# Layer 2's harmonics transposed two groups ahead, and a prologue that loads its edges by group

## The chip, the cores and the metric

The kernel runs on one core of a Trainium2 chip. The core has five engines with an instruction queue each: TensorE (PE, matmuls and transposes, with weight loads PEld beside them), VectorE (DVE), ScalarE (ACT), GpSimd (POOL) and SyncE (SP, which here only issues DMAs). The time is the device time of one execution in microseconds, as a median over runs. Besides, one execution was recorded by the hardware profiler; every single duration below is from that execution.

## The reference

Four graph layers run one after the other on the same graph: N = 12500 nodes of 128 features, E = 212500 edges, sorted by destination. Each layer takes h = relu(layernorm(x)) and adds its result to x.

```python
def reference(x, src, dst, edge_attr_16, edge_attr_9, edge_weight, edge_weight1, ...):
    h = jnp.maximum(_layernorm(x), 0.0)
    x = x + _L0(h, edge_index, edge_attr_16, ...)
    h = jnp.maximum(_layernorm(x), 0.0)
    x = x + _L1(h, edge_index, edge_weight1, ...)
    h = jnp.maximum(_layernorm(x), 0.0)
    x = x + _L2(h, edge_attr_9, edge_index, ...)
    h = jnp.maximum(_layernorm(x), 0.0)
    x = x + _L3(h, edge_index, ...)
    return x

# layer 0: attention. Wh = h @ W.T in 4 heads of 32
attn = leaky_relu((concat(Wh[src], Wh[dst]) * a).sum(-1)) + edge_feat @ W_e.T
alpha = softmax of attn over the edges of each dst
out = layernorm(gelu(segment_sum(alpha * Wh[src], dst)))
# layer 1: gelu(gelu(segment_sum(h[src] * edge_attr, dst)) @ W.T + b)
# layer 2: tensor product with 9 spherical harmonics per edge, five paths (i1, i2, io)
tmp = einsum('eui,ej,ijk->euk', x1[i1], x2[i2][:, 0, :], CG[p])
msg = einsum('euk,uw->ewk', tmp, weights[p]) * alpha
out = zeros.at[dst].add(msgs)
# layer 3: mean of relu(h)[src] over each dst, two matmuls, batch norm over the nodes
```

In layer 2 the node row of 128 is one block of 32 scalars and one of 32 vectors of 3.

## The kernel before

The edges are cut into NG = 208 groups of GE = 1024, each as 128 partitions with T = 8 slots. Because the edges are sorted by destination, a group's destinations lie in a short window of nodes. A group is summed by a one-hot matrix: `rel` is the destination less the group's first one (`base`), the one-hot compares it with the columns 0 to 127, held in PSUM as `iop` (L176 to L178), and a matmul with the one-hot as one operand adds the edges' rows into the window's nodes. An edge's source row is fetched by an indirect DMA on POOL's queue, one per slot, so 8 per group (`gather`, L730; L738 is a variant that spaces them out, used in layers 1 and 3).

**Prologue.** The table loop (from L238) normalizes x in 25 batches of rows, transposes them on PE (L252), multiplies by `WE` (L260) and writes table `tab0`, from which layer 0 gathers; `rows0` loads the batches eight ahead into nine buffers of `xt`. `sdall` becomes the table `sdt` (L276 and the store ahead of it). Then the edges: `load_edges` (L123) brings dst and src into [partition, group, slot], 8 indices of 4 bytes in each piece (`di`, `si`). Extremes of each group come from reductions over the slots and a reduction over the partitions on POOL (L331), and from them `base`, `rel` (L335) and several index tables. `dpad` is a padded copy of dst in DRAM, read back as `seq` in shifted rows, which gives the sortedness check `bad` and the unit counts `units` (matmul `pun`, L386). `rough` (L402) collects whatever would break the kernel's assumptions. Last, `rel16`, a copy of `rel` in group order and bf16, is made by 13 transposes (L408), 13 copies and 13 stores (L411). Weights follow (L424, L429, L446).

**Layer 0.** Its loop does for a group `load` (the edge features, `rb` from rel16 L1019, `sdw` from sdt L1023), `logits` (gather into X, one of LAG + 8 = 15 buffers; transpose of the features L1032, copy eT L1034, matmuls, the logit sums), and LAG groups later, after the softmax over windows (`weights`), `spread_out` (msg L1112, matmuls L1116) and `add_up` (L1120).

**Layer 2.** The order is written out by hand (`tc.manual_schedule`). Per group: `mix` transposes the 9 harmonics of 8 slots on PE (pyT, L1334), copies them on ACT (eT, L1336) and multiplies by `mixer` on PE (mix, L1337), which gives 15 coefficients per edge. `window2` is a generator that is advanced step by step: 8 scalings on ACT (A, L1350); the one-hot on DVE (L745); 8 tensor operations on DVE with the coefficients (L1355 to L1367, called BC here); 8 matmuls on PE (pag, L1372) and the copy R on ACT (L1374); 3 transposes on PE (pT, L1377); the addition into acc on DVE (L1380). Iteration g issues mix(g+1), then for its own group the gathers, A, the one-hot and BC, then acc(g-3), pag and R of g-1, and pT of g-2. X has 11 buffers; `py`, with both the transposed harmonics and the coefficients, has 2. `Nodes` adds, every other group or so, the node work of finished windows (L590 to L622). So on PE the order is pyT(g+1), mix(g+1), pag(g-1), pT(g-2); on ACT eT(g+1), A(g), node work, R(g-1).

`feature_stream` (L798) holds the edge features in blocks of 4 groups and loads a block when its first group asks for it:

```python
            if b not in held:
                held.clear()
                g1 = min((b + 1) * per, NG)
                held[b] = sp.tile([P, per, T * k], F, name=name)
                load_edges(held[b], v, b * per, g1, 0.0, k)
```

Of the kernel before, what the change touches and what calls it, by code (L numbers as in the profile page):

```python
# [26 lines left out]
P = 128  # L27
T = 8
# [65 lines left out]
def gnn_kernel(ctx: ExitStack, tc, x, src, dst, ef16, ef9, ew, W0, We0, a0, lns, lnb, W1, b1,  # L94
# [81 lines left out]
    cps = ctx.enter_context(tc.tile_pool(name="cps", bufs=1, space=PSUM))  # L176
    iop = cps.tile([P, W], F, name="iop")
    vec.tensor_copy(iop, io)  # L178
# [24 lines left out]
    tmp = early.enter_context(tc.tile_pool(name="acp", bufs=1))  # L203
    sp, pp = (pre.enter_context(p) for p in (tc.tile_pool(name="p0", bufs=3),
# [3 lines left out]
    def rows0(k):  # L208
        if k < NK:
            b0, nb = k * NBK, min(NBK, NB - k * NBK)  # L210
            xs0[k] = sp.tile([P, nb, D], F, name="xt", bufs=9)
            load_rows(xs0[k], x, b0, nb)

    NK = -(-NB // NBK)
    for k in range(8):
        rows0(k)
    with tc.tile_pool(name="wt0", bufs=1) as wp, tc.tile_pool(name="wtp0", bufs=1, space=PSUM) as pw_:
# [13 lines left out]
        vec.tensor_copy(WE[:, P:], aps)  # L231
    sdall = sp.tile([P, NB, H], F, name="sdall", bufs=1)
    for k in range(NK):
# [19 lines left out]
        hT = sp.tile([P, nb, P], F, name="hT")  # L253
# [10 lines left out]
        rows0(k + 8)  # L264
# [14 lines left out]
    si = cst.tile([P, NG, T], I, name="si")  # L279
# [12 lines left out]
    TOT = PADF + NG * GE + P  # L292
# [6 lines left out]
    with tc.tile_pool(name="ed", bufs=1) as ep:  # L299
        di = ep.tile([P, NG, T], I, name="di")  # L300
        load_edges(di, dst, 0, NG, N, 1)
        load_edges(si, src, 0, NG, 0, 1)
        df = ep.tile([P, NG, T], F, name="df")
        vec.tensor_copy(df, di)

        ends = ep.tile([1, max(PADF, TOT - PADF - E)], I, name="ends")
        vec.memset(ends, -1)
        nc.sync.dma_start(dpad[None, :PADF], ends[:, :PADF])
        ends2 = ep.tile([1, TOT - PADF - E], I, name="ends2")
        vec.memset(ends2, N)  # L310
        nc.sync.dma_start(dpad[None, PADF + E :], ends2)
        cut = max(k for k in range(1, P + 1) if E % k == 0)
        nc.sync.dma_start(dpad[PADF : PADF + E].rearrange("(a b) -> a b", a=cut), dst.rearrange("(a b) -> a b", a=cut))
        ext = ep.tile([P, 2, NG + 1], F, name="ext")
        vec.memset(ext[:, :, NG:], 0.0)
        vec.tensor_reduce(ext[:, 0, :NG], df, AX.X, ALU.max)
        vec.tensor_reduce(ext[:, 1, :NG], df, AX.X, ALU.min)
        vec.tensor_scalar_mul(ext[:, 1, :NG], ext[:, 1, :NG], -1.0)

        seq = [ep.tile([P, NG * T], I, name=f"seq{k}") for k in (0, 1, 2)]  # L320
        for t, k in zip(seq, (0, 1, HALO)):
            nc.sync.dma_start(t, windows(dpad, PADF + k, P, NG * T, NG * T))
        bad = [ep.tile([P, NG * T], F, name=f"bad{k}") for k in (0, 1)]
        vec.tensor_tensor(bad[0], seq[2], seq[0], ALU.is_le)
        vec.tensor_scalar(bad[1], seq[0], float(N), None, op0=ALU.is_lt)
        vec.tensor_tensor(bad[0], bad[0], bad[1], ALU.mult)
        vec.tensor_tensor(bad[1], seq[1], seq[0], ALU.is_lt)
        vec.tensor_tensor(bad[0], bad[0], bad[1], ALU.max)
        vec.tensor_reduce(ext[:, 0, NG:], bad[0], AX.X, ALU.max)
        red = ep.tile([P, 2, NG + 1], F, name="red")  # L330
        pool.partition_all_reduce(red, ext, P, bass_isa.ReduceOp.max)  # L331
        base = ep.tile([P, NG], F, name="base")
        vec.tensor_scalar_mul(base, red[:, 1, :NG], -1.0)
        vec.tensor_copy(bi, base)
        vec.tensor_tensor(rel, df, base[:, :, None].to_broadcast([P, NG, T]), ALU.subtract)  # L335
        vec.tensor_scalar(widx, base, pcol, None, op0=ALU.add)
        span = ep.tile([P, NG], F, name="span")
        vec.tensor_tensor(span, red[:, 0, :NG], base, ALU.subtract)
        vec.tensor_copy(xall, span)
        vec.tensor_scalar(xall, xall, 7, None, op0=ALU.logical_shift_right)  # L340
        vec.tensor_scalar(xall, xall, 1.0, None, op0=ALU.add)
        vec.tensor_scalar(bi3, base, float(BM), None, op0=ALU.min)
        vec.tensor_scalar(bir, bi, RW - 1, None, op0=ALU.bitwise_and)

        last = base[:, G0 - GM : G0, None].to_broadcast([P, GM, T])
        vec.tensor_tensor(relx, rel[:, G0 - GM : G0, :], last, ALU.add)
        vec.tensor_scalar(relx, relx, W0_ * P - 0.5, 4.0 * P, op0=ALU.is_gt, op1=ALU.mult)
        vec.tensor_tensor(relx, relx, rel[:, G0 - GM : G0, :], ALU.add)
        most = ep.tile([P, 1], F, name="most")
        vec.tensor_reduce(most, span, AX.X, ALU.max)  # L350
        worst = ep.tile([P, 1], F, name="worst")
        vec.scalar_tensor_tensor(worst, red[:, 0, NG:], float(W), most, op0=ALU.mult, op1=ALU.max)

        least = ep.tile([P, NG], F, name="least")
        pool.memset(least, 0.0)
        for k, g in enumerate(done):
            if g + 1 < NG:
                pool.memset(least[:, g + 1 :], float(min(NBK * P * (k + 1), N)))
        pool.memset(least[:, G0:], float(W0_ * P))
        for k, g in enumerate(done):  # L360
            if g + 1 >= G0 and g + 1 < NG:
                pool.memset(least[:, g + 1 :], float(min(NBK * P * (k + 1), N)))
        vec.tensor_tensor(least, base, least, ALU.is_lt)

        end = ep.tile([P, NG], F, name="end")
        pool.memset(end, float(RW - W))
        for k, g in enumerate(done):
            if g + 6 < NG:
                pool.memset(end[:, g + 6 :], float(NBK * P * (k + 1) + RW - W))
        vec.tensor_tensor(end, base, end, ALU.is_gt)  # L370
        vec.tensor_tensor(least, least, end, ALU.max)

        UP = NG * T // P
        edge = ep.tile([P, 2, NW], F, name="edge")
        vec.tensor_copy(edge[:, 0, :], wnode)
        vec.tensor_scalar(edge[:, 1, :], wnode, float(P), float(N), op0=ALU.add, op1=ALU.min)
        below = ep.tile([P, 2, NW, UP], F, name="below")
        for k, at in enumerate((P - 1, 0)):
            unit = seq[0].rearrange("p (u e) -> p u e", e=P)[:, :, at]
            vec.tensor_tensor(below[:, k], unit[:, None, :].to_broadcast([P, NW, UP]),  # L380
                              edge[:, k, :, None].to_broadcast([P, NW, UP]), ALU.is_lt)
        units = ep.tile([P, 2, NW], F, name="units")
        vec.tensor_reduce(units, below, AX.X, ALU.add)
        with tc.tile_pool(name="bgp", bufs=1, space=PSUM) as pp:
            pun = pp.tile([P, 2, NW], F, name="pun")
            pe.matmul(pun.rearrange("p k w -> p (k w)"), ones, units.rearrange("p k w -> p (k w)"),  # L386
                      start=True, stop=True)
            vec.tensor_scalar(begin, pun[:, 0, :], float(P), float(E - UN * P), op0=ALU.mult, op1=ALU.min)
            vec.tensor_copy(units[:, 1, :], pun[:, 1, :])
            vec.tensor_tensor(units[:, 0, :], units[:, 1, :], pun[:, 0, :], ALU.subtract)  # L390
        vec.tensor_scalar(units[:, 0, :], units[:, 0, :], UN + 0.5, None, op0=ALU.is_gt)
        many = ep.tile([P, 1], F, name="many")
        vec.tensor_reduce(many, units[:, 0, :], AX.X, ALU.max)
        vec.scalar_tensor_tensor(worst, many, float(W), worst, op0=ALU.mult, op1=ALU.max)
        vec.tensor_scalar(many, base[:, G0 - 1 : G0], BM + 0.5, None, op0=ALU.is_gt)
        vec.scalar_tensor_tensor(worst, many, float(W), worst, op0=ALU.mult, op1=ALU.max)
        vec.tensor_scalar(many, red[:, 0, G0 - GM - 1 : G0 - GM], W0_ * P - 0.5, None, op0=ALU.is_gt)
        vec.scalar_tensor_tensor(worst, many, float(W), worst, op0=ALU.mult, op1=ALU.max)
        late = ep.tile([P, 1], F, name="late")
        vec.tensor_reduce(late, least, AX.X, ALU.max)  # L400
        vec.scalar_tensor_tensor(worst, late, float(W), worst, op0=ALU.mult, op1=ALU.max)
        vec.tensor_copy(rough, worst)  # L402
        relf = rel.rearrange("p g t -> p (g t)")
        with tc.tile_pool(name="edp", bufs=2, space=PSUM) as pp:
# [587 lines left out]
    with (tc.tile_pool(name="e0", bufs=2) as sp, tc.tile_pool(name="e0p", bufs=2, space=PSUM) as pp,  # L992
# [129 lines left out]
        with tc.manual_schedule():  # L1122
# [46 lines left out]
            while nodes.step(NG + LAG + 2):  # L1169
                pass  # L1170
            slots.close()


    def tabled1(sp, pp, tabS, make):

# [645 lines left out]
```

## Time and profile before

| what | us |
|---|---|
| median of 4 runs | 9673.07 (9665.19 to 9674.17) |
| the profiled execution | 9670.84 |
| its span | 9669.0 |
| prologue, to the first gather of layer 0 | 170.6 |
| layer 0, to its last pag | 3368.7 |
| layer 1 and what lies between | to about 5150 |
| layer 2 | about 5150 to 7966 |
| layer 3 | the rest |
| busy: PE, PEld, DVE, ACT, POOL | 5156.2, 3242.7, 5346.7, 2808.2, 5146.3 |

The span is read in order of time. The stages follow each other, since each gathers from the table that the one before wrote. No engine is busy for more than 55% of the span (DVE), so a share over the whole span does not name a bound; each stage is read by itself, by its waits and its timeline. In the lists below a line of a timeline is: start, duration (us), engine, line, operation, out<-in, shape, count, and in brackets the idle time of the engine just ahead and what ended it. A line of a wait list is: engine, tile and line that waited, <- what released it: us in total, times, longest. "remote" stands for a releaser that the records do not explain. SPq is the DMA queue that SP issues to.

### The profile page before, as it was taken

How to read it: one execution, taken by the hardware profiler on the slowest of the kernel's cores; microseconds unless marked ns; L12 is line 12 of the kernel's file. 1: busy time of each engine (PE TensorE's matmuls, PEld its weight loads, DVE VectorE, ACT ScalarE, POOL GpSimd, SP SyncE). 2: the span in 40 equal slices, each digit the busy share in tenths (PEclk: the TensorE clock that was granted, in tenths of full speed). 3: DMA queues.
4: the chain of work that ended last, by engine and by line, in shares of the span. 5: the costliest groups of instructions: out<-in, count | busy, mean ns of one | idle time of the engine just before them, and what ended most of it. 6: DMA issues, size and time to landing. Idle time of an engine off the chain costs nothing. (4 is left out here: it accounts for less than half of the span.)

```text
span 9669.0 us, 105443 instructions
## 1 busy us (share of the span) xinstructions
PE 5156.2 (53%) x33167; PEld 3242.7 (34%) x33168; DVE 5346.7 (55%) x10302; ACT 2808.2 (29%) x7509; POOL 5146.3 (53%) x5434
## 2 busy tenths in 40 slices
PE   2233333333333328788883555555555564777776
PEld 2233333332333215555552333333333331222222
DVE  4465665665566613334343777777777772444443
ACT  2133332333333303333332222222222221333333
POOL 2554555555545166666634555555555526665662
PEclk6565555555556658888886777777777786888887
DMA  7232222232223222222221111111111114333333
GB/s 104 64 76 71 75 74 73 74 76 72 73 72 77 48 78 72 75 76 76 74 64 52 45 52 51 50 55 50 51 52 51 53 32 121 87 88 84 87 88 91
DMA packets 740838, 673.63 MB, mean 70 GB/s; under 512 B 340899, under 2 KB 629014, under 8 KB 740247
## 3 DMA queue, kind: packets, MB, share of 16 engines
q0 software_dynamic: 186624, 382.17, 15.0%
q1 hardware_dynamic: 553643, 284.63, 11.7%
q8 instruction: 262, 4.29, 0.2%
q14 instruction: 309, 2.53, 0.1%
HBM read 603.91 MB, written 63.28 MB: 69 GB/s over the span
## 5 line engine op out<-in xcount | busy, mean ns | idle before, releaser
L730 POOL DMA_INDIRECT X<-tab,si x1664 | 1615.5, 971 | 1463.4 <-DVE msg L1112 676.3
L730 POOL DMA_INDIRECT X<-htab,si x1664 | 1576.3, 947 | 1131.4 <-ACT prods L1350 583.6
L738 POOL DMA_INDIRECT X<-htab,si x968 | 939.9, 971 | 630.4 <-PE pag L1309 219.0
L738 POOL DMA_INDIRECT xg<-tab,si x968 | 921.1, 952 | 649.5 <-issue 230.2
L1372 PE MATMUL pag<-prods,oh 128*128 128x352 f32 x3328 | 1237.4, 534 | 0.0
L1116 PE MATMUL pag<-oh,msg 128*128 128x128 f32 x3328 | 724.9, 406 | 328.8 <-DVE msg L1112 277.9
L1372 PEld LDWEIGHTS pag<-prods,oh 128*128 128x128 f32 x3328 | 739.9, 229 | 411.3 <-issue 180.0
L1337 PE MATMUL py<-mixer,eT 72*128 72x120 f32 x416 | 131.3, 408 | 1234.2 <-ACT eT L1336 1066.6
L1116 PEld LDWEIGHTS pag<-oh,msg 128*128 128x128 f32 x3328 | 671.5, 308 | 344.2 <-DVE msg L1112 281.4
L1510 ACT CAST xb<-px 128x384 bf16<-128x384 f32 x1050 | 491.8, 480 | 1006.2 <-PE px L1499 337.2
L1036 PE MATMUL pt<-WeB,eT 128*128 128x32 f32 x416 | 124.2, 390 | 1108.0 <-ACT eT L1034 815.6
L1246 ACT ACTIVATE xs<-px,wslot 128x128 f32<-128x128 f32 x1050 | 371.4, 366 | 1150.2 <-PE px L1234 474.8
L1374 ACT COPY R<-pag 128x352 f32<-128x352 f32 x208 | 94.1, 452 | 1905.6 <-remote 1223.4
L1234 PE MATMUL px<-tabS,oha 128*32 128x128 f32 x8652 | 518.4, 315 | 212.9 <-issue 108.3
L1499 PE MATMUL px<-tabS,oha 128*32 128x384 bf16 x4326 | 441.8, 395 | 305.2 <-issue 195.7
L1215 PE MATMUL pw<-ohb,xs 128*128 128x128 f32 x2100 | 578.7, 362 | 18.8 <-ACT xs L1246 12.5
L1309 PE MATMUL pag<-oh,X 128*128 128x128 f32 x1936 | 443.7, 319 | 213.3 <-issue 123.0
L1337 PEld LDWEIGHTS py<-mixer,eT 72*128 72x128 f32 x416 | 82.9, 249 | 1295.2 <-ACT eT L1336 1108.5
L1350 ACT ACTIVATE prods<-X,ef 128x128 f32<-128x128 f32 x1664 | 510.3, 393 | 12.4 <-DMA X<-htab,si 12.1
L1036 PEld LDWEIGHTS pt<-WeB,eT 128*128 128x128 f32 x416 | 97.1, 290 | 1183.1 <-ACT eT L1034 865.5
L1380 DVE TENSOR_TENSOR acc<-acc,pT 128x384 f32 x208 | 114.5, 550 | 678.9 <-remote 655.0
L1105 ACT ACTIVATE oh<-iop,far 128x128 f32<-128x128 f32 x1664 | 452.9, 383 | 41.1 <-DVE ohj L948 32.7
(463 smaller groups left out, 10265.9 us busy)
## 6 DMA issues: line engine op xcount, KB each, us to landing
lob<-lo SPq DMA_DIRECT2D x252, 224.0 KB
rb<-rel SPq DMA_DIRECT2D x208, 256.0 KB
X<-htab,si POOLq DMA_INDIRECT x2632
X<-tab,si POOLq DMA_INDIRECT x1664
xtab<-xv SPq DMA_DIRECT2D x72, 256.0 KB
xv<-xtab SPq DMA_DIRECT2D x72, 256.0 KB
xg<-tab,si POOLq DMA_INDIRECT x968
lob<-lo SPq DMA_DIRECT2D x84, 160.0 KB
```

Source lines behind the costliest of these rows:

```text
L730: pool.indirect_dma_start(out=t[:, s, :], out_offset=None, in_=table[:, :], in_offset=bass.IndirectOffsetOnAxis(ap=idx[:, s : s + 1], axis=0))
L738: pool.indirect_dma_start(out=ts[-1][:, : table.shape[1]], out_offset=None, in_=table[:, :], in_offset=bass.IndirectOffsetOnAxis(ap=idx[:, ...
L1105: act.activation(S[:, t, :], iop, AF.Abs, bias=far[:, t : t + 1])
L1116: pe.matmul(pag, msg[:, t, :], S[:, t, :], start=t == 0, stop=t == T - 1)
L1215: pe.matmul(pw, x, b, start=j == 0, stop=j == NT - 1)
L1234: pe.matmul(px[q * SL : (q + 1) * SL, :], a[:, jj * P + q * SL : jj * P + (q + 1) * SL], tabS[:, blk, :], start=True, stop=True)
L1246: act.activation(x, px, AF.Copy, scale=by)
L1309: pe.matmul(p, r[t], s[:, t, :], start=t == 0, stop=t == T - 1)
L1350: act.activation(A[:, t, :], X[:, t, :], AF.Copy, scale=e[:, t, 0:1])
L1372: pe.matmul(pag, S[:, t, :], prods[:, t, :], start=t == 0, stop=t == T - 1)
L1499: pe.matmul(px[q * SL : (q + 1) * SL, :], a[:, jj * P + q * SL : jj * P + (q + 1) * SL], tabS[:, blk, :], start=True, stop=True)
L1510: act.copy(x[:, : 3 * P], px)
```

## The change

Four parts.

1. **Layer 2.** `mix` becomes a generator `turn` of three steps: transpose, copy, matmul. Iteration g now does the matmul of g+1, whose transpose and copy are done already, then the transpose of g+2, and, as its last step behind R(g-1), the copy of g+2. `py` gets three buffers. The PSUM for it comes from `iop`, which is closed for this layer and put beside `part` (the products in BC) in one PSUM tile `own`; it is made again ahead of layer 3.
2. **Prologue.** dst and src are loaded as rows of one group each (4 KB) in [112 | 96 x 1024], turned into slots on PE (`slots_of`), src ahead of the table loop, dst behind it. Extremes are reductions over the row, spread to all partitions by a matmul of ones with a diagonal (`pr`). `rel16` is written by two stores from ACT's casts. The padded copy is stored first; the sortedness check works in bf16 and stands last. The x ring has 7 buffers, loaded six ahead.
3. **Layer 0's X** has a pool of its own (`xr`), made ahead of the prologue's pools and closed behind layer 0.
4. **`feature_stream`** loads a block of four groups ahead (layers 0 and 2).

The diff, cut to its core:

```diff
@@ constants @@
-    cps = ctx.enter_context(tc.tile_pool(name="cps", bufs=1, space=PSUM))
-    iop = cps.tile([P, W], F, name="iop")
-    vec.tensor_copy(iop, io)
+    held_ = ctx.enter_context(ExitStack())
+    def columns(name):
+        t = held_.enter_context(tc.tile_pool(name=name, bufs=1, space=PSUM)).tile([P, W], F, name="iop")
+        vec.tensor_copy(t, io)
+        return t
+    iop = columns("cps")
...
+    rows_ = ExitStack()
+    xr = rows_.enter_context(tc.tile_pool(name="xr", bufs=LAG + 8))
...
-            xs0[k] = sp.tile([P, nb, D], F, name="xt", bufs=9)
+            xs0[k] = sp.tile([P, nb, D], F, name="xt", bufs=7)
...
-    for k in range(8):
+    for k in range(6):
         rows0(k)
@@ ahead of the table loop @@
+    gd = [ep.tile([n, GE], I, name=f"gd{c}") for c, n in enumerate(HN)]
+    gs = [ep.tile([n, GE], I, name=f"gs{c}") for c, n in enumerate(HN)]
...
+    for t, v in ((gs, src), (gd, dst)):
+        m = HN[1] // 16 * 16 - 16
+        for c, a, b in ((0, 0, HN[0]), (1, 0, m), (1, m, HN[1] - 1)):
+            nc.sync.dma_start(t[c][a:b], v[(HB[c] + a) * GE : (HB[c] + b) * GE].rearrange("(g e) -> g e", g=b - a))
+        nc.sync.dma_start(t[1][HN[1] - 1 : HN[1], :tail], v[None, (NG - 1) * GE :])
+    def slots_of(out, t, c):
+        n = HN[c]
+        for q in range(0, T, 4):
+            ps = ppt.tile([P, 4, HN[0]], F, name="pst")[:, :, :n]
+            for k in range(4):
+                pe.transpose(ps[:, k, :], t[:, q + k :: T], ident[:n, :n])
+            vec.tensor_copy(out[:, HB[c] : HB[c + 1], q : q + 4].rearrange("p g t -> p t g"), ps)
...
+    for c in (0, 1):
+        gsf = ep.tile([HN[0], GE], F, name="gf", bufs=2)[: HN[c]]
+        vec.tensor_copy(gsf, gs[c])
+        slots_of(si, gsf, c)
@@ behind the table loop @@
-        load_edges(di, dst, 0, NG, N, 1)
-        load_edges(si, src, 0, NG, 0, 1)
...
-        pool.partition_all_reduce(red, ext, P, bass_isa.ReduceOp.max)
...
-                pe.transpose(prl[:n, :], relf[:, c : c + n], ident)
-                rl = ep.tile([P, P], B16, name="rl", bufs=2)
-                vec.tensor_copy(rl[:n, :], prl[:n, :])
-                nc.sync.dma_start(rel16[c : c + n, :], rl[:n, :])
...
+        for c in (0, 1):
+            vec.tensor_copy(gf[c], gd[c])
+            n = HN[c]
+            vec.tensor_reduce(ext[:n, c, 0:1], gf[c], AX.X, ALU.min)
+            vec.tensor_reduce(ext[:n, c, 1:2], gf[c], AX.X, ALU.max)
+            for k in (0, 1):
+                dg = ep.tile([P, P], F, name="dg", bufs=2)[:n, :n]
+                vec.tensor_scalar(dg, ident[:n, :n], ext[:n, c, k : k + 1], None, op0=ALU.mult)
+                pe.matmul(pr[:, k, HB[c] : HB[c + 1]], ones[:n, :], dg, start=True, stop=True)
+            vec.tensor_scalar(gf[c], gf[c], ext[:n, c, 0:1], None, op0=ALU.subtract)
+        vec.tensor_copy(red, pr)
...
+        act.copy(r16, gf[c].rearrange("g (p t) -> g t p", t=T))
+        nc.sync.dma_start(rel16[HB[c] * T : HB[c + 1] * T, :].rearrange("(g t) p -> g (t p)", t=T),
+                          r16.rearrange("g t p -> g (t p)"))
+        slots_of(rel, gf[c], c)
...
+        pe.matmul(pbd, ones, anybad, start=True, stop=True)
@@ feature_stream @@
-            if b not in held:
-                held.clear()
-                g1 = min((b + 1) * per, NG)
-                held[b] = sp.tile([P, per, T * k], F, name=name)
-                load_edges(held[b], v, b * per, g1, 0.0, k)
+            held.pop(b - 1, None)
+            for c in (b, b + 1):
+                if c not in held and c * per < NG:
+                    held[c] = sp.tile([P, per, T * k], F, name=name)
+                    load_edges(held[c], v, c * per, min((c + 1) * per, NG), 0.0, k)
@@ layer 0, logits @@
-            X = xs[g] = sp.tile([P, T, P + H], F, name="X", bufs=LAG + 8)
+            X = xs[g] = xr.tile([P, T, P + H], F, name="X")
@@ layer 2 @@
-        def mix(g):
+        def turn(g, deep=2):
             e = feats(g)
-            py = pp.tile([P, 2, P], F, name="py")
+            py = pp.tile([P, 2, P], F, name="py", bufs=deep)
             pe.transpose(py[: T * 9, 0, :], e, ident)
+            yield
             eT = sp.tile([T * 9, P], F, name="eT")
             act.copy(eT, py[: T * 9, 0, :])
+            yield
             pe.matmul(py[:, 1, : T * NY], eT, mixer, start=True, stop=True)
...
+    held_.close()
...
+        own = pp.tile([P, 1024], F, name="own", bufs=1)
+        iop = own[:, T * 3 * HD : T * 3 * HD + W]
+        vec.tensor_copy(iop, io)
...
-            mixed[0] = mix(0)
+            for k in (0, 1):
+                turns[k] = turn(k, 3)
+                next(turns[k])
+                next(turns[k])
+            mixed[0] = next(turns.pop(0))
             g = -1
             while nodes.step(g := g + 1) or g < NG + 3:
                 if g + 1 < NG:
-                    mixed[g + 1] = mix(g + 1)
+                    mixed[g + 1] = next(turns.pop(g + 1))
+                if g + 2 < NG:
+                    turns[g + 2] = turn(g + 2, 3)
+                    next(turns[g + 2])
                 if g < NG:
                     going[g] = window2(...)
                     step(g)
                 step(g)
                 step(g)
                 step(g - 3)
                 step(g - 1)
                 step(g - 2)
+                if g + 2 < NG:
+                    next(turns[g + 2])
+    iop = columns("cps3")
```

## The prediction

> **What bounds the kernel now.** I read the page's chain of waits first, then the waits of the stage that the change rewrites most (layer 2, 5150 to 7970 us), then a stretch of its timeline, and last the queues of the prologue.
>
> The chain names no engine as the bound; its largest entry is time that no instruction on record explains:
>
> ```profile
> another core or an unknown queue 16%; PE 16%; issue 7%; ACT 5%; DVE 2%; DMA 0%; POOL 0%; DVEq 0%; ACTq 0%; SPq 0%; POOLq 0%
> ```
>
> The table of waits in layer 2 (engine, line, what was waited for: us in total, times, longest) says where that time sits. "remote" stands where the recorded releaser had long been done:
>
> ```profile
> ACT R L1374 <- remote: 1223.4, 86, 46.3
> ...
> DVE acc L1380 <- remote: 655.0, 99, 44.2
> POOL X L730 <- ACT prods L1350: 583.6, 93, 19.0
> ...
> ACT eT L1336 <- remote: 180.6, 54, 10.2
> ```
>
> All three "remote" waits are for PE: R copies pag, acc adds pT, eT copies py. The timeline of one such wait (start, us, engine, line), engine by engine:
>
> ```profile
> 6600.41 4.91 PE L1372 MATMUL pag<-prods,oh 128*128 128x352 f32 x16
> 6605.48 0.27 PE L1334 MATMUL py<-ident,ef 128*72 128x128 f32 x1
> 6617.19 0.78 PE L1337 MATMUL py<-mixer,eT 72*128 72x120 f32 x2 [11.44 <-ACT eT L1336]
> ...
> 6616.01 0.45 ACT L1374 COPY R<-pag 128x352 f32<-128x352 f32 x1 [13.62 <-remote]
> 6616.88 0.26 ACT L1336 COPY eT<-py 72x128 f32<-72x128 f32 x1
> ...
> 6616.06 0.56 DVE L1380 TENSOR_TENSOR acc<-acc,pT 128x384 f32 x1 [6.76 <-remote]
> ...
> 6612.19 0.95 POOL L730 DMA_INDIRECT X<-htab,si  x1 [0.30 <-issue]
> ```
>
> pag ended at 6605.32, and its reader R began at 6616.01; from 6609.3 ACT, DVE and PE all stood still. POOL alone worked, gather behind gather with 0.3 us between, to 6613.14; 2.9 us later everything moved. I read this so: while POOL issues gathers back to back, word that PE is done reaches ACT and DVE late, about 3 us after the run of gathers ends. The windows (PE, PEld, DVE, ACT, POOL busy, clock, DMA share, GB/s) agree:
>
> ```profile
> 6606.00:6616.00 10.00, 0.00 (x0) 0.00 (x0) 3.20 (x4) 0.00 (x0) 5.61 (x6) 0.70 0.17 47
> ...
> 7860.00:7970.00 110.00, 78.70 (x286) 50.66 (x286) 91.73 (x120) 32.87 (x105) 0.20 (x1) 0.86 0.04 11
> ```
>
> With no gathers left (7860 on) DVE is 83% busy and R follows pag at once. So groups go in pairs: 16 gathers at 0.95 + 0.30 = 1.25 us are 20 us, some 3 us of late word, and 3.7 us of R, eT, node work and A (L1350, 8 scalings, 2.45 us), for which POOL waits since A frees the X buffers; 26 us per pair, 13.0 us per group (77 groups between 6000 and 7000). In the timeline POOL pauses 101 times in the layer, 649 us in all, 6.4 us each.
>
> The start of layer 0 is the other place. SP's queue, POOL's first gather and two copies on ACT:
>
> ```profile
> 20.02 14.76 SPq L150 DMA_DIRECT2D tab<-tt  x3
> ...
> 51.24 15.54 SPq L150 DMA_DIRECT2D tab<-tt  x1
> ...
> 116.48 21.48 SPq L150 DMA_DIRECT2D sdt<-s  x2
> 138.62 13.36 SPq L411 DMA_DIRECT2D rel<-rl  x13
> ...
> 170.61 1.30 POOL L730 DMA_INDIRECT X<-tab,si  x1 [53.59 <-DVE cut_s L1009]
> ...
> 262.23 0.27 ACT L1034 COPY eT<-pt 128x128 f32<-128x128 f32 x1 [83.92 <-issue]
> 339.23 0.27 ACT L1034 COPY eT<-pt 128x128 f32<-128x128 f32 x1 [76.73 <-remote]
> ```
>
> The two stores at 20.02 and 51.24 stand behind the loads of di and si (issued 17.05 and 49.87, pieces of 32 bytes) and block SP; DVE waits 19.7 us for tab<-tt in all. The first gather comes at 170.6, released by a memset of layer 0, though tab0's last store was issued at 107. Then 15 groups are gathered in one run (to 320.9), in which eT passes only at 178, 262 and 339. The first msg is at 370.8; from there a group takes 15.0 us.
>
> **The change, part by part.**
>
> *Transposes two groups ahead (layer 2).* Operations per group are the same. PE's order was pyT(g+1), mix(g+1), pag(g-1), pT(g-2); now mix(g+1), pyT(g+2), pag(g-1), pT(g-2). ACT's cyclic order stays R, eT, A, with node work now behind eT. What goes is eT's wait for PE: its pyT is older than the pag that R, just ahead of it, already waited for; before, pyT stood behind pT, which itself waits for acc. I followed eT through the timeline: it began over 0.3 us after its predecessor 59 times, 203.6 us in all; in 120.4 us of these POOL was idle too, in the rest it was still gathering and the wait lay beside that. I take 120, bounds 0 (R's late word sets the pair anyway) and 204. mix now waits for an eT of the iteration before, so pag starts behind R at once, not behind eT and mix (1.76 us in the rows above, 6616.01 to 6617.77); that is off POOL's path, and I price it 0. What is late next is R itself (1223 us of "remote") and acc: the change leaves both behind PE. The wait that is added, mix on eT(g+1), has pag queued behind it on PE and R behind that, but its eT is an iteration old. The third py buffer is paid for by putting iop beside part in one PSUM tile; DVE reads and writes both, in order, price 0. iop is rebuilt twice by one copy (one_hot's 128x1024 takes 1.22 us): under 3 us.
>
> The trace page of the Trainium skill speaks against my reading of "remote": Perfetto Trace Analysis, Tensor Engine Instruction, has the update pushed when PSUM acknowledges the bytes, and then propagated, with no word of waiting for another engine. With prompt word (as after 7860) layer 2 would be bound by DVE at about 10 us a group and eT's move would be worth nothing; the 10.7 us between 6605.32 and 6616.01 decide, and I keep 120.
>
> *Prologue.* Edges come by group in 8 loads of 4 KB rows rather than 32-byte pieces; src is turned on PE ahead of the table loop (2 casts of 1024 at 1.22 us, 4 copies at about 0.6: 4.8 us of DVE). The table loop is paced by ACT at 2.45 us for each of 25 batches, so the 19.7 us of stall should go: 107 - 20 + 5 = 92 for the last table store. X's buffers are now made ahead of the prologue, so the first gather needs si and tab0 only: about 94 instead of 170.6, and the run of 120 gathers (150 us) ends near 244 instead of 320.9. But dst's part of the prologue (red<-pr, four slot copies, pun, pbd, three weights: ten PE handoffs) now falls into that run, where such handoffs took 84 and 77 us. On SP the sdt store of 21.5 us stays; 13 rel16 stores become 2. Best: all of this passes beside the run, msg(0) at 244 + 50 (370.8 - 320.9) = 294, gain 77. Worst: all of it follows the run, 64 us more (107 to 171), gain 13. By the two eT rows two handoffs pass in the run and eight wait, some 30 us of DVE work (30.0 busy in 107 to 171) after it: msg(0) near 325, gain 45. The x ring of 7 rather than 9 is covered by six batches ahead, 6 x 2.45 = 15 us; uncovered it costs a load's few us, once.
>
> *Edge features a block ahead.* PE waited 2.8 us for ef in layer 2: 0. It adds no DMA, only earlier ones.
>
> Sum against the profiled run (9670.8, span 9669.0): 9670.8 - 120 - 45 = 9506. The median of the runs is 2 above the profiled run: 9508, rounded to 9505.
>
> By the clock rule (TensorE: Matmul & The Clock Gate, Part 1: half rate after an idle window of about 3.4 us) each pair still starts cold, since the run of gathers stays; the rows say so too (0.70 in the idle window). Warm, pag would gain, but POOL does not wait for it: by either, 0.
>
> **The rivals.**
> (a) *Layer 2 gains nothing:* R's release, 3 us after the gathers, is the only gate, and eT falls in step behind it. For: eT is 180.6 us of "remote" against 1223 of R. Against: the 120 us with POOL idle. 9673 - 45 = 9628.
> (b) *More:* with eT out of the way half of POOL's 649 us of pauses goes, 325, and the start gives 60: 9288. Against: the pause holds R and A in any case.
> (c) *Slower: pairs break.* A pair holds because R(g) gets its word in the first 4 to 5 us of the next run of gathers. If A, let go sooner, starts POOL sooner relative to pag, R misses that and each group pays its own pause: 3.0 + 3.7 = 6.7 us for each pause more. From 165 / 6.7 = 25 pauses more (126 instead of 101) it eats the whole gain; at 140 it is 39 x 6.7 = 261, 9673 + 261 - 165 = 9769. Against: pag starts 1.2 us sooner as well.
> (d) *It doesn't do what it says:* handoffs in the prologue hang until the run ends and layer 2 stays as it is: 9660 to 9673.
>
> **How the numbers follow.** Forecast 0.47 (its own range 9420 to 9580), (a) 0.20, (b) 0.10, (c) 0.16, (d) 0.07. Faster by over 0.2% (19 us, about what a measurement of this kernel can tell from no change) hold the forecast, (a) and (b): 0.77; same (d): 0.07; slower (c): 0.16. The range runs from all upper bounds together (9670.8 - 204 - 77 = 9390) to the near edge of (c), 9700; it leaves out most of (b) and of (c), 2 in 10.
>
> **What would show it.** Right: no "remote" entry of note for eT in layer 2; POOL's pauses still about 100 but near 5.2 us; R's "remote" still over 1000 us; first gather near 94, first msg near 325, no 15 us store on SP ahead of it; layers 1 and 3 of unchanged length. Wrong: a first gather beyond 130 or a first msg beyond 360; 126 pauses or more in layer 2; acc or R taking over what eT gave; layer 2's DVE over 90% busy, which would mean that late word was not the bound.

## The result, and the profile after

The changed kernel takes 9695.37 us (median of 38 runs, 9650.93 to 9733.58); the kernel before, measured with it, 9663.95 (61 runs, 9630.36 to 9686.89). The ratio is 1.003, 95% interval 1.0023 to 1.0037: slower by 0.3%, where 1.7% faster was forecast. The profiled execution of the changed kernel has a span of 9707.2 us.

By stages, from the two traces: first gather of layer 0, first msg, then the lengths from the first msg to that of group 190, from there to the last pag of layer 0, and of layer 2 (first mix to last acc):

| us | first gather | first msg | msg 0 to 190 | 190 to end | layer 2 |
|---|---|---|---|---|---|
| before | 170.6 | 370.8 | 2798.9 | 199.0 | 2816.8 |
| after | 93.0 | 310.4 | 2826.3 | 241.3 | 2830.4 |

The start is 60 us ahead. By the end of layer 0 these are gone, and layer 2, which was to be 120 us shorter, is 14 longer. The stretch between layers 0 and 2 and the one behind layer 2 add 6 and 9 us. The start in the timeline of the changed kernel (start, us, engine, line; SP, POOL, ACT and DVE one after the other):

```profile
13.43 1.80 SPq L258 DMA_DIRECT2D gs<-in_src_dram  x3
...
20.04 1.62 SPq L150 DMA_DIRECT2D tab<-tt  x2
...
92.59 22.72 SPq L150 DMA_DIRECT2D sdt<-s  x2
...
92.95 1.32 POOL L770 DMA_INDIRECT X<-tab,si  x1 [23.98 <-DMA TP<-in_L_gnn_weights_dram]
...
152.03 0.27 ACT L1074 COPY eT<-pt 128x128 f32<-128x128 f32 x1 [27.00 <-PE pt L1072]
266.98 0.27 ACT L1074 COPY eT<-pt 128x128 f32<-128x128 f32 x1 [114.68 <-remote]
...
310.43 1.22 DVE L1152 TENSOR_TENSOR msg<-X,alp 128x1024 f32<-128x1024 f32 x1
```

The table stores no longer stand 15 us on SP, the gathers start at 93, ACT stands still for 115 us ahead of one copy of a PE result, which passes only behind the long run of gathers (120 of them, to 249.7), and the first msg is at 310.

Where the time goes shows in POOL's timeline, changed kernel first, kernel before second. In both, the line is the fill of the last block of edge features, which has only part of its edges (L134, in `load_edges`), in layer 0 and in layer 2:

```profile
3145.89 0.21 POOL L134 MEMSET ef<- 128x128 f32 x1 [89.63 <-PE pt L1072]
...
7718.54 0.95 POOL L770 DMA_INDIRECT X<-htab,si  x1 [0.30 <-issue]
7792.73 0.16 POOL L134 MEMSET ef<- 128x72 f32 x1 [73.24 <-ACT prods L1398]
```

```profile
3179.45 0.20 POOL L134 MEMSET ef<- 128x128 f32 x1 [43.84 <-PE pt L1032]
...
7808.97 0.16 POOL L134 MEMSET ef<- 128x72 f32 x1 [28.22 <-ACT prods L1350]
```

POOL stands still for 89.6 and 73.2 us instead of 43.8 and 28.2, with all later gathers behind it: the fill waits for the last reader of the buffer that the block takes over, and one block ahead that reader is four groups further off. In layer 2 the waits (window 5150 to 7970, changed kernel) are:

```profile
ACT R L1422 <- remote: 1330.7, 86, 58.7
...
DVE acc L1428 <- remote: 512.5, 69, 47.7
POOL X L770 <- ACT prods L1398: 420.4, 71, 15.7
...
POOL ef L134 <- ACT prods L1398: 73.2, 1, 73.2
```

eT has left the list of "remote" waits (180.6 us before), as it should; R has 107 us more of them.

### The profile page after: what moved, and what is told of

The parts are those of the page before. It is cut to its first block, busy times and chain, and to the rows that moved or that the text cites. A ratio compares the mean times of both kernels' runs of the same rounds, so it can differ in the third digit from the quotient of the medians.

```text
span 9707.2 us, 105216 instructions
## 1 busy us (share of the span) xinstructions
PE 5169.4 (53%) x33196; PEld 3253.9 (34%) x33197; DVE 5342.2 (55%) x10307; ACT 2803.8 (29%) x7511; POOL 5157.4 (53%) x5435
```

## The experiments

The runs fell on several chips, of two kinds: the kernel before takes 9552, 9556 and 9559 us on three of them (9664 in the measurement above), and 7295 and 7304 on two. Ratios are against the kernel before on the same chip; a comparison across chips of one kind goes by ratios and stage lengths.

**The parts, one at a time** (before: 9551.91). `e1` takes the feature stream back; `e2` has it alone; `e4` has layer 2's order and the shared PSUM tile alone, `e5` the prologue and the early X alone:

```diff
# e1, against the changed kernel; e2 is the reverse, against the kernel before
-            held.pop(b - 1, None)
-            for c in (b, b + 1):
-                if c not in held and c * per < NG:
-                    held[c] = sp.tile([P, per, T * k], F, name=name)
-                    load_edges(held[c], v, c * per, min((c + 1) * per, NG), 0.0, k)
+            if b not in held:
+                held.clear()
+                g1 = min((b + 1) * per, NG)
+                held[b] = sp.tile([P, per, T * k], F, name=name)
+                load_edges(held[b], v, b * per, g1, 0.0, k)
# e4, against the kernel before: the change's parts for iop, layer2 and its loop
+            mixed[g + 1] = next(turns.pop(g + 1))
...
# e5, against the kernel before: the change's parts ahead of layer 0, and X
+            X = xs[g] = xr.tile([P, T, P + H], F, name="X")
...
```

> The changed kernel with the feature blocks loaded as before (each block when its first group asks for it); prologue, early X and layer 2 as changed. Theory A (the loss is the fill of the last, partial feature block on POOL, which with the block ahead waits 89.6 us in layer 0 and 73.2 us in layer 2 at the head of the gathers' queue, against 43.8 and 28.2 before): the ends of layers 0 and 2 come some 43 and 40 us earlier than in the changed kernel, 9695 - 83 = about 9612; the two waits are back at about 44 and 28 us. Rival B (the new order or the shared PSUM tile of layer 2 costs the time): no change, about 9690. Rival C (the prologue's early gathers are paid back in layer 0 whatever the features do): 9650 to 9670.

> The kernel before with the block-ahead feature loads alone. Theory A: slower by about 83 us, 9664 + 83 = about 9747, with POOL's waits ahead of the fills near 90 and 73 us. Rivals B and C: within 20 us of 9664, since neither layer 2's order nor the prologue is in it. My prediction's price for this part was 0.

> The kernel before with layer 2's new order and the shared PSUM tile alone. Prediction's price: 120 us faster, 9544. Theory A with late word passing from eT to R (in the changed kernel's trace layer 2 was only 14 us ahead before the fill): 15 to 30 us faster, 9634 to 9649. Rival B: slower than 9664 by 20 us or more.

> The kernel before with the new prologue and the early X pool alone. Prediction's price: 45 us faster, 9619. In the changed kernel's trace the first msg came 60 us sooner and 30 us were left of it at group 190. If what was lost in between came from the feature loads (SP waits for a buffer still read): 60 us kept, 9604. If it is lost in layer 0 anyway: 30 us, 9634. Rival C: 0 to 15 us, 9650 to 9664.

| run | us | ratio (95%) | first msg | msg 0 to 190 | 190 to end | layer 2 |
|---|---|---|---|---|---|---|
| e1 old features | 9475.86 | 0.9921 (0.9907 to 0.9935) | 313.9 | 2750.5 | 201.0 | 2760.7 |
| e2 only features | 9675.68 | 1.0123 (1.0107 to 1.0139) | 372.8 | 2791.0 | 241.2 | 2813.2 |
| e4 only layer 2 | 9537.75 | 0.9978 (0.9961 to 0.9996) | 370.8 | 2760.4 | 200.0 | 2762.3 |
| e5 only prologue | 9501.46 | 0.9943 (0.9931 to 0.9955) | 316.0 | 2754.6 | 200.9 | 2787.4 |

The change without its feature stream is 76 us faster; the feature stream alone costs 118 (0.0123 x 9552), more than the 83 that were expected, and 0.9921 x 1.0123 = 1.0043 is close to the 1.003 of the whole. The stages place it: 241 instead of 200 from group 190 on (41 us), 2813 instead of 2787 in layer 2 (26 us; both have the old order), and 31 to 40 us between msg 0 and msg 190, which the fill, standing at the very end, cannot explain. What the edit adds there is on SP, in the waits of e2 in layer 0 (600 to 3000 us); whether it costs the time is tested further down (g1):

```profile
SPq L128 <- remote: 461.1, 24, 30.5
SPq L128 <- PE pt L1032: 262.6, 14, 25.2
```

L128 is the load of a full block. It waits 19 us in the mean, in 38 blocks, by the program for the transposes of the block whose buffer it takes over (the rows name them 14 times and leave 24 unexplained); rb, sdw and the logits' stores queue behind it. With the old stream (e1, e4, e5) the list has no such wait. Layer 2's order is worth 25 to 27 us in its stage (2787.4 against 2762.3 and 2760.7), the prologue 50 in all (interval 43 to 66).

**SP's wait and POOL's fill apart.** `e3` loads only full blocks ahead; `e6` goes back to the old stream and gives the last block a tile of its own, filled and loaded at the first use of the stream. `e9` and `e10` put a fill into a tile that nobody reads behind each gather of layer 2 (old stream, all else as changed), to test my reading of "remote": a rest between gathers.

```diff
# e3, against the changed kernel
-            for c in (b, b + 1):
+            for c in (b, b + 1) if (b + 2) * per <= NF else (b,):
# e6, against e1
+            last = (NG - 1) // per
+            if "last" not in held:
+                t = held["last"] = sp.tile([P, per, T * k], F, name=name + "z", bufs=1)
+                load_edges(t, v, last * per, NG, 0.0, k)
+            if b == last:
+                return held["last"][:, g - b * per, :]
-                held.clear()
+                held.pop(b - 1, None)
# e9, e10, against e1, in rows2: the 8 gathers written out, and behind each
+                    pool.memset(rest, 0.0)     # rest is [P, 8] in e9, [P, 256] in e10
```

> The changed kernel, but the last, partial block of features is not loaded ahead; the full blocks are. Two costs of the feature loads are in question: POOL's fill of the last block (some 41 us in layer 0 and 25 in layer 2), and SP's wait ahead of each block's load in layer 0 for a buffer that is still read (724 us in 38 waits in the run with the features alone, with rb, sdw and the logits' stores queued behind). If the fill is all, the ratio to the kernel before is that of the run with the old loads, 0.992. If SP's waits cost the 31 us that layer 0 lost by group 190, it is about 0.992 + 31 / 9552 = 0.9955, with the ends of both layers moved by the fill's share alone. Rival: neither, 1.003.

> The changed kernel with the old, one-block loads and a tile of its own for the last, partial block, filled and loaded when the stream is first used. If POOL's wait ahead of the fill holds the gathers and nothing else takes its place, the 42.7 us of layer 0 and 38.7 us of layer 2 that are left in the run with the old loads go too: its ratio 0.992 less up to 81 / 9552 = 0.0085, so 0.984 to 0.988. If the X buffers or DVE hold POOL at that place anyway: 0.992.

> The run with the old loads (ratio 0.992), and behind each gather of layer 2 a fill of 128 x 8 on POOL into a tile that nobody reads (0.105 us each for such a fill in the profile before, so some 1.4 us from gather to gather instead of 1.25, 11.3 us per group). If PE's word is late because the gathers follow each other without a rest, and this rest suffices: R's remote waits fall well below 1000 us and a group takes 11.3 to 12 us instead of 13, ratio about 0.965 to 0.98. If the word is late whatever the rest: pairs of 22.6 + 3 + 3.4 = 29 us, 1.5 us more per group, 0.992 + 208 * 1.5 / 9552 = 1.025.

> As the run with short rests, but the fills are 128 x 256 (0.205 us for 128 x 128 in the profile before, so about 0.4 us; some 1.65 us from gather to gather, 13.2 us per group). If the word is prompt with such rests, POOL sets the pace at 13.2 us with no pauses: near 0.995, R's remote waits under 300 us, DVE and ACT without common stops. If the word stays late: pairs of 26.4 + 6.4 = 33 us, 16.4 per group, 0.992 + 208 * 3.4 / 9552 = 1.066.

These four fell on the first chip of the fast kind (before: 7294.51), where no word is late, so that what was expected of them doesn't apply: e3 0.9948 (0.9936 to 0.9960), e6 0.9929 (0.9915 to 0.9944), e9 0.9956 (0.9940 to 0.9971), e10 1.0366 (1.0350 to 1.0382). Another chip of that kind (7303.84) had the changed kernel itself beside them.

> The changed kernel as it is, on the chip of this batch. On a chip where PE's word is late behind POOL's gathers (the kernel before near 9600 us): 1.003 again, POOL's waits ahead of the fills near 90 and 73 us. On one where the word is prompt (before near 7295, no pauses of POOL in layer 2): if the loss is the features' alone, it stands above the run with full blocks ahead (0.995 there) by the fill of the last block, about 40 us of 7295, so near 1.000; if the loss needs late word, near 0.995.

> As the run of the same kernel before it (full blocks ahead, the last one not), for a chip with late word: SP's waits alone give 0.9955, the fill alone gives 0.992, neither gives 1.003. On a chip with prompt word 0.995 again.

> As the run of the same kernel before it (old loads, the last block in a tile of its own). With late word: 0.984 to 0.988 if POOL's wait ahead of the fill is all that holds the gathers there, 0.992 if not. With prompt word 0.993 again.

> As the run of the same kernel before it (a small fill behind each gather of layer 2). On the chip with prompt word the fill fitted into the 0.30 us between gathers (1.257 from gather to gather instead of 1.25). With late word: if the word waits for the gathers to pause, a rest this short changes nothing, pauses near 85, R's remote waits above 1000 us, 0.992; if a foreign instruction between gathers lets it pass, R's waits fall and layer 2 comes under 12 us a group, below 0.975.

Changed kernel 0.9995 (0.9986 to 1.0004), full blocks ahead 0.9957 (0.9944 to 0.9970), last block apart 0.9928 (0.9915 to 0.9940), short rests 0.9960 (0.9945 to 0.9974). So on these chips the last block ahead costs 7297.44 - 7271.86 = 26 us and the change as a whole comes out even. Part of why these chips are 24% faster shows in layer 2. Waits of the run with the last block apart (3800 to 5850 us):

```profile
ACT R L1428 <- PE pag L1426: 1031.8, 188, 12.8
PEld pT L1431 <- DVE acc L1434: 654.1, 195, 7.6
```

No "remote" is left for R: in all 208 groups it starts within 2 us of the end of pag, 0.09 us after it in the median. On the other kind it is over 2 us late 94 times in the kernel before. The gather's pace is the same (0.946 us each, 1.25 from one to the next), but POOL never pauses for over 1 us: the layer takes 10.1 us a group instead of 13.1 to 13.6. So R's delay of the first profile is a matter of the chip. It is not all of the difference: from the end of layer 0 to layer 2 this run takes 1367 us and the kernel before, on its chip, 1781; behind layer 2 it is 1380 against 1702. There the gathers are spaced out, and no run tried rests. The granted clock is higher too (0.80 against 0.71 over the span), but a matmul of pag takes 523 ns instead of 534, and PE's whole busy time is only 316 us less (4840 against 5156), of 2431.

Then a chip of the late kind again (9556.02), with full blocks ahead, the last block apart, and long rests:

> For a chip with late word (the kernel before near 9550 to 9670): the changed kernel without the last block ahead. SP's waits alone cost 31 us: 0.9955, layer 0 steady part about 31 us longer than with the old loads, the ends of the layers without the 41 and 25 us of the fill. Fill alone: 0.992. On a chip with prompt word 0.9955 as twice before.

> For a chip with late word: no wait of POOL ahead of a fill is left. 0.984 to 0.988 if that wait alone holds the gathers there, 0.992 if the X buffers take its place. On a chip with prompt word 0.993 as twice before.

> For a chip with late word: 128 x 256 fills between the gathers of layer 2, 1.44 us from gather to gather and 11.6 us per group on the other chip, without pauses there. If a rest of 0.5 us between gathers lets PE's word pass, R's remote waits are gone and a group takes 11.6 to 12 us instead of 13.3: 0.992 - 208 * 1.5 / 9552 = 0.96. If the word waits for a pause whatever the rests: pairs of 23 + 6.5 us, 14.8 per group, 0.992 + 208 * 1.5 / 9552 = 1.025.

| run | us | ratio (95%) | first msg | msg 0 to 190 | 190 to end | layer 2 |
|---|---|---|---|---|---|---|
| g1 full blocks ahead | 9544.27 | 0.9985 (0.9968 to 1.0003) | 319.1 | 2803.0 | 199.0 | 2770.4 |
| g2 last block apart | 9440.74 | 0.9880 (0.9859 to 0.9900) | 327.3 | 2766.0 | 157.9 | 2731.7 |
| g3 long rests | 9149.89 | 0.9579 (0.9557 to 0.9600) | 312.8 | 2753.0 | 198.9 | 2433.0 |

g1 keeps SP's wait (2803 against 2766) and loses the fill's (199 as before). Its ratio stands 0.0064 above e1's: SP's share is some 60 us (by the two intervals 39 to 83), 37 of them in layer 0 up to group 190 against g2, or 50 against g3 below, whose layer 0 is that of e1. SP's waits cost more than was expected of them (a ratio of 0.9955). The fill's share is 1.003 - 0.9985, some 43 (25 to 61). Without any wait at the fill both ends shrink once more, by 43 and 29 us: the kernel before pays for that fill too. POOL's waits ahead of the fills, g2 first, e2 second:

```profile
POOL efz L134 <- DMA sdt<-s: 51.4, 1, 51.4
POOL efz L134 <- ACT g L616: 18.8, 1, 18.8
```

```profile
POOL ef L134 <- PE pt L1032: 89.6, 1, 89.6
POOL ef L134 <- ACT prods L1350: 66.9, 1, 66.9
```

In g2 both lie ahead of the layers' first gathers. Part of the wait is slack there: in layer 0 the first gather is 27 us later than in e1 (121 against 94), the first msg 13.

g3 is the largest step of the study. Windows of 5500 to 6500 us in g2 and in g3 (PE, PEld, DVE, ACT, POOL busy, clock, DMA share, GB/s), and ACT's group for R in each:

```profile
5500.00:6500.00 1000.00, 573.35 (x1950) 368.58 (x1949) 759.28 (x951) 247.69 (x819) 594.54 (x628) 0.78 0.21 53
...
L1428 ACT COPY R<-pag 128x352 f32<-128x352 f32 x208 | 94.0, 452 | 1993.7 <-remote 1422.1 <-PE pag L1426 334.7 <-issue 187.8
```

```profile
5500.00:6500.00 1000.00, 659.60 (x2161) 435.93 (x2160) 841.23 (x1060) 297.83 (x902) 883.60 (x1383) 0.81 0.23 59
...
L1428 ACT COPY R<-pag 128x352 f32<-128x352 f32 x208 | 93.9, 452 | 930.0 <-PE pag L1426 466.3 <-issue 310.7 <-remote 102.9
...
6000.93 0.33 POOL L1375 MEMSET rest<- 128x256 f32 x1
6001.42 0.95 POOL L1372 DMA_INDIRECT X<-htab,si  x1 [0.16 <-issue]
6002.37 0.33 POOL L1375 MEMSET rest<- 128x256 f32 x1
```

The same gathers, each followed by a fill of 0.33 us and so 1.44 us apart instead of 1.25, and R's "remote" falls from 1422 to 103 us, the gaps of over 1 us between gathers from 91 to 4, a group from 13.1 to 11.7 us. On the fast kind of chip the same rests make the kernel slower (e10): there POOL's pace is the bound, and nothing is late.

**Rests in layer 0 too.** The fill behind each gather of layers 0 and 2, on top of g2 in two sizes, and on the kernel before:

```diff
-    def gather(t, table, idx):
+    def gather(t, table, idx, rest=None):
...
+            if rest is not None:
+                pool.memset(rest, 0.0)     # [P, 128] in h1, [P, 256] in h2 and h3
```

> The changed kernel with old loads and the last block in its own tile (0.988 with late word), and behind each gather of layers 0 and 2 a fill of 128 x 128 (0.205 us; some 1.31 us from gather to gather, 10.5 us per group). If a rest of 0.36 us lets the word pass as one of 0.48 did: layer 2 at 10.5 to 11 us a group instead of 13.2 (some 480 us), layer 0 at 11 instead of 14.8 (some 750): 0.988 - 1230 / 9552 = 0.86. If it doesn't: R's waits stay above 1000 us, 0.985 to 1.0. With prompt word: 0.995 to 1.005.

> The same with fills of 128 x 256 (1.44 us from gather to gather). With late word: layer 2 as in the run with long rests (327 us less than without), layer 0 at about 11.8 us a group instead of 14.8, some 600 us: 0.988 - 930 / 9552 = 0.89. If layer 0's pace is not set by late word (DVE's msg holds POOL there): 0.953. With prompt word: slower, 1.04 to 1.08.

> The kernel before with fills of 128 x 256 behind each gather of layers 0 and 2, nothing of the change. With late word: as the run above plus what the prologue and layer 2's order give (0.012): 0.90, or 0.965 if layer 0 does not answer. With word prompt, the new order of layer 2 should be worth nothing: the two runs with the same rests differ by the prologue's 50 us and the fill's 80 at most.

Late kind (9558.67): h1 9253.83, 0.9676 (0.9651 to 0.9701); h2 8535.57, 0.8924 (0.8902 to 0.8946); h3 8592.88, 0.8991 (0.8969 to 0.9014). So layer 0 is set by late word as well: 2436 us from the first msg to its end in h2, against 2924 in g2, and its longest "remote" entry (window 600 to 2200, g2 first, h2 second) falls with it:

```profile
ACT eT L1080 <- remote: 346.7, 41, 21.9
```

```profile
ACT eT L1083 <- remote: 50.6, 13, 7.5
```

The rest has to be long: at 1.33 us from gather to gather (h1, between its two forecasts) layer 2 still has 73 gaps of over 1 us between gathers, and R waits over 2 us 78 times. So it isn't any instruction between two gathers that lets the word pass; the shortest fill, which leaves the pace at 1.25 us, ran only where no word is late (e9, f4). h2 beats both kernels by 11% on this kind of chip. And with the word mostly prompt the new order of layer 2 is worth little: 2433 us in h2, 2440 in h3.

## Why the prediction was wrong, point by point

**The step that failed: the edge features a block ahead, priced at 0 because it "adds no DMA, only earlier ones".** It cost 118 us by itself (e2), and turned a gain of 76 into a loss. What I left out is what the forecast asks of every moved step: each queue that it is moved past, and POOL's fill is an instruction too. The earlier load takes over a buffer whose readers are not done. On SP it waits 19 us a block ahead of rb and sdw (some 60 us of time, by g1); on POOL the fill of the one partial block waits 90 and 73 us ahead of the gathers (41 and 26 us by the stages). I looked at who waits for ef, which is nobody, and not at what the load itself waits for.

**Layer 2's order, priced at 120, brought 26** in its stage (the old order in e5, the new one in e4 and e1). The mechanism was right as far as eT goes: its "remote" waits are gone. But the pause did not end with them, since R waits for the same late word. I count a gap of over 1 us between two gathers as a pause. Before, R began within 2.5 us of POOL's last gather in 27 of 86 pauses behind 16 gathers, and eT in none. After, in 77 pauses behind 16 or 24 gathers, R did so 18 times and eT 16 times. Only these 16 became shorter, 4.8 us in the median instead of 6.3; in 59 of the other 61 R, too, began later than that, and R took eT's place. That is close to rival (a), which I had at 0.20. I counted every overlap of eT's wait with an idle POOL as time to be had, and the 120 was too high already as a count: 24 us of it are the 0.30 us that lie between any two gathers, and only 96 fall into pauses.

**The start of layer 0, priced at 45, was right:** first gather 93 (94 expected), first msg 310 (325), 50 us in the time (e5). From the end of the first run of gathers to the first msg it took 61 us instead of 81; which of the ten handoffs made the difference was not looked at. The tab stores that stood 15 us behind the 32-byte loads are gone. The Trainium skill (DMA: Bandwidth & Descriptors, Specifications) puts the least transfer for full rate at 512 B; 32-byte pieces lie below it and 4 KB rows above it, and the SP lines agree, though no run changes the size of the pieces alone.

**The reading of "remote" held as far as it was tested, and was used too narrowly.** That the run of gathers holds R up is shown by g3 and h2, where rests end it. The page that I set against it (Perfetto Trace Analysis, Tensor Engine Instruction) has the update pushed once PSUM has acknowledged the bytes, and then propagated; on two of the chips R does follow pag by 0.09 us. The rows of the others don't refute it: a matmul's end in this profile is modelled, so they can't tell whether PE's write or the word of it was late, and "late word" is a name for the delay between pag's recorded end and R. Having found that a run of gathers without rests holds up every engine, I took it as given and priced only what the change did around it.

**The rivals:** slower it was, but not by (c). Pairs did not break into single groups: runs of 8 gathers fell from 13 to 7, and 18 runs of 24 appeared where there had been one. So layer 2 has 86 pauses of over 1 us instead of 101, but they are no shorter, 654 us against 649, with the fill's 73 us instead of 28 among them. None of the rivals had the feature stream in it.

## What to carry to other kernels

A prefetch is priced by what it waits for, not by who waits for it: a load one block earlier needs a buffer that is free one block earlier, or it stops the queue that it stands in. That holds for every instruction of the load, also a fill for one partial block on another engine; give such a block a tile of its own. And where a profile shows several engines stopped together, test the stop itself before pricing what is around it: a fill of 0.33 us behind each gather brought the ratio from 0.9880 (g2) to 0.8924 (h2), some 900 us, the change without its feature stream 76 us. That holds for chips on which the word is late; on the others the same fill in layer 2 made the kernel 3.7% slower than the one before (e10).

## What the runs showed of the hardware

- Two kinds of chip: the same kernel takes 9552 to 9664 us on some and 7295 to 7304 on others, with the same gather durations (0.95 us) and pace (1.25 us). In layer 2 they differ in how soon R follows pag's recorded end while POOL issues gathers: 0.09 us in the median and never over 2 us on one kind, over 2 us in 94 of 208 groups on the other. The stretches with spaced gathers are shorter on the fast kind as well (1367 against 1781 us, 1380 against 1702); why was not looked for.
- On the late kind the pace of the gathers decides: at 1.25 and 1.33 us from one to the next the word is late, at 1.44 us it mostly is not. Where between 1.33 and 1.44 it turns was not looked for, nor was the cause; why chips differ stays open.
- A load one block ahead into two buffers made SP wait 19 us a block, in 38 blocks, for readers of the buffer; the fill of the partial block made POOL wait 90 and 67 us ahead of its gathers (e2).
